# Recurrent gates split by feature chunk into two PSUM banks, with products of 32 columns

## The chip, the core and the metric

The kernel runs on one core of a Trainium2 chip. The metric is device time in microseconds. The core has a matrix engine (TensorE, PE in the profile; its weight loads are listed as PEld), a vector engine (VectorE, DVE), an activation engine (ScalarE, ACT), GpSimd (POOL) and a queue engine that issues DMAs (SyncE, SP). Matrix products are written to PSUM, an accumulation memory of banks of 2 KB per partition; the engines' other data is in SBUF. All numbers are float32.

## The reference

The input x has 8 sequences of 512 positions with 256 features. Four layers follow one another, each adding its output to its input: a mixture of experts with one shared and eight routed experts, a layer that for this depth comes to a per-sequence gain, a low-rank adapted block, and a gated recurrence. The recurrence is what the change is about. Its state has 256 features for each of the 8 sequences, and it runs over 512 positions one after the other:

```python
def step(H, xs):
    xz, xr, xh = xs
    Z = jax.nn.sigmoid(xz + H @ Whz.T + bhz)
    R = jax.nn.sigmoid(xr + H @ Whr.T + bhr)
    H_tilda = jnp.tanh(xh + R * H @ Whh.T + bhh)
    H_new = Z * H + (1.0 - Z) * H_tilda
    Y = H_new @ Whq.T + bhq
    return (H_new, Y)
```

R must be known before the candidate's product, and the candidate before the next state.

## The kernel before, in words

**Windows and steps.** The first three layers are worked in 16 windows of 32 positions (all 8 sequences, so 256 columns). Their products, activations and vector operations are jobs in lists, one for each engine. Two windows are done ahead; then the recurrence starts, and the jobs of the later windows are put between its instructions. A written planner does that while the program is built: at fixed places in each step a `jobs.fill` takes the next job that is ready by the planner's own clock (a step counts 2.43 us there). What comes out is one fixed order for each engine[...]. The recurrence's step is written out in the loop over c (32 time chunks of 16 positions) and t.

**One step.** TensorE multiplies the state by the r weights (`recur`, L1117 in `across`), then by the z weights. ScalarE applies the sigmoid to r in two parts (`gate`, L1298), one for each feature chunk of 32 columns. VectorE turns each part over in blocks of 32 by 32 (`transposed`, L1312) and multiplies by the state (L1329, s_rh). TensorE then makes the candidate's product from s_rh, ScalarE its tanh in two parts, VectorE turns each part over (d) and makes the new state with a scan, one for each chunk (L1388, s_h). z goes the same way beside this, in one part of 64 columns. ScalarE also copies each state into a history (L1402) from which the output is made later.

**Layout of the gates.** The 256 outputs of a gate lie as four strips of 32 partitions with 64 columns each. For each strip j, `across` multiplies a stationary operand of 32 columns (4 positions by 8 sequences) with 64 columns of the weights. A gate takes 2 feature chunks of the input by 4 strips, 8 products of 64 columns. In the trace each is two weight loads and two passes, so that a gate shows 16 of each.

**Banks.** r and the candidate of one time chunk share a bank, `grh`: 4 groups of 4 positions, 2 gates, 64 columns. Two such banks alternate from time chunk to time chunk. z has a third bank, `gz`, for both. Before a bank's first use `claim` (L300) writes it with eight products of zeros, so that the later products add to what is there. Then ScalarE copies the biases into it (`biases`, L1139), in two halves for r and candidate and one part for z; for the next time chunk it does so in steps 7, 8 and 9. The input's products (wx) are added by `project`: for each group of 4 positions, in four parts, r and candidate together in one product of 128 columns for each strip, z in one of 64. The parts with r and candidate stand before the candidate's products of every second step.

**Bank reuse.** The second `grh` bank first serves small products of the other layers' preparation (the ring `r_c`), and is claimed in step 4 of the first time chunk. `implied` leaves out waits that another engine's order already gives. Where ScalarE copies the z bias into the bank that z products write, the next z products do wait for it (`z_bias`).

Of the kernel before, what the change touches and what calls it, by code (L numbers as in the profile page):

```python
# [9 lines left out]
F32 = mybir.dt.float32  # L10
AF = mybir.ActivationFunctionType
ALU = mybir.AluOpType
AX = mybir.AxisListType
PSUM = bass.MemoryType.PSUM
DRAM = bass.MemoryType.DRAM

P = 128
B, T, C = 8, 512, 256
KC = C // P
# [13 lines left out]
FQ = C // NQ  # L33
GS = 4
NG = TC // GS
# [165 lines left out]
def cond_resid_kernel(  # L201
# [44 lines left out]
    def implied(later, *earlier):  # L246

        for e in earlier:
            tc.declare_no_dep(later.ins, e.ins, reason="through another engine")
# [9 lines left out]
    def pool_of(name, bufs, space=None):  # L259
        kw = {} if space is None else {"space": space}  # L260
        return ctx.enter_context(tc.tile_pool(name=name, bufs=bufs, **kw))
# [18 lines left out]
    r_xt = ring("xt", [P, KC, WS, B], 3)  # L280


    ps_g = pool_of("ps_g", 2, PSUM)
    ps_z = pool_of("ps_z", 1, PSUM)
    gz = ps_z.tile([P, 2, NG, FQ], F32, name="gz")

    def new_gates(c):
        rh = ps_g.tile([P, NG, 2, FQ], F32, name=f"grh_{c}", tag="grh")
        return rh, gz[:, c % 2]

    both = [new_gates(c) for c in range(2)]
    zeros = const.tile([P, NT], F32, name="zeros")
    nc.vector.memset(zeros, 0.0)
    rh0, rh1 = [g[0].rearrange("p n g f -> p (n g f)") for g in both]

    def claim(bank):

        for half in range(2):
            for j in range(NQ):
                nc.tensor.matmul(  # L300
                    bank[ts(j, 32), ts(half, NT)],
                    zeros[:, 0:32],
                    zeros,
                    start=half == 0,
                    stop=half == 1,
                    skip_group_check=True,
                )
# [4 lines left out]
    jobs = Jobs()  # L312
# [70 lines left out]
    r_c = Ring(None, "c", None, 1, rh1)  # L383
    pieces = {}
    for pair_ in LOW:
        for k in range(KC):
            for q in pair_:
                z = Lazy(r_w2)
                pieces[q, k] = (z, load(z, w2[ts(k, P), ts(q, R * C)], 1.0, [z]))

    wx = const.tile([P, KC, 3, C], F32, name="wx")
    wh = const.tile([P, KC, 4, C], F32, name="wh")
    for g, n in enumerate((0, 2, 1)):
        got_wx = load(wx[:, :, g, :], rows_of(sq_b[:, ts(n, C)]), 0.25)
    for j in range(NQ):
        got_wh = load(
            wh[ts(j, 32)].rearrange("q i n o -> q i (n o)"),
            sq_b[ts(j, FQ), 3 * C : 7 * C].rearrange("(i q) o -> q i o", q=32),
            0.25,
        )  # L400
# [3 lines left out]
    got_small = []  # L404
# [42 lines left out]
    for n in range(2):  # L447
        u = const.tile([P, NT], F32, name=f"u{n}")
# [285 lines left out]
    def pe(fn, deps, lazies=(), takes=0.3):  # L734
        return jobs.add("PE", fn, deps, lazies, takes)
# [7 lines left out]
    def flat(z):  # L743
# [5 lines left out]
    j = dve(  # L749
        lambda: tt(  # L750
            prod,
            rout[:, 1].rearrange("p k (o e) -> p k o e", o=1).broadcast_to([P, KC, B, E]),
            cond.rearrange("p k (b o) -> p k b o", o=1).broadcast_to([P, KC, B, E]),
            ALU.mult,
        ),
        [got_cond, got_rout],
    )
# [12 lines left out]
    j = pe(time_bias, [j], [tb_ps])  # L770
# [15 lines left out]
    for n in range(2):  # L786
        t = const.tile([P, B, 32], F32, name=f"gates{n}")
# [112 lines left out]
    mu, j = mean_over_features(cond, got_cond)  # L900
    diff = set1.tile([P, KC, B], F32, name="diff")

    def center():
# [3 lines left out]
    j = dve(center, [j], [mu], 0.4)  # L907
    dsq = set1.tile([P, KC, B], F32, name="dsq")
    j = dve(lambda: tt(dsq, diff, diff, ALU.mult), [j])
    var_ps, j = mean_over_features(dsq, j)  # L910
    var = set1.tile([P, B], F32, name="var")
    j = dve(
        lambda: nc.vector.tensor_scalar(var, var_ps.get()[:, :B], EPS_LN, None, ALU.add),
        [j],
        [var_ps],
    )

    sd0 = set1.tile([P, B], F32, name="sd0")
    j = act(lambda: nc.scalar.activation(sd0, var, AF.Sqrt), [j], (), 1.6)
# [57 lines left out]
    hid_pre, j = dense_cond(A_L2W1, lnc, V_BIAS1, "hid", got_lnc)  # L977
    hid_e, j = gated(hid_pre, AF.Erf, RSQRT2, "hid_e", j)
# [10 lines left out]
    g1_pre, j = dense_cond(A_L1W1, cond, V_B1, "g1", got_cond)  # L989
    g1, j = gated(g1_pre, AF.Sigmoid, 1.0, "g1", j)  # L990
    j = dve(lambda: tt(g1, g1, g1_pre, ALU.mult), [j])
    gate_pre, j = dense_cond(A_L1W2, g1, V_B2, "gate", j)
# [9 lines left out]
    for n, of in enumerate(LOW):  # L1002
# [59 lines left out]
            0.35,  # L1062
        )

    xts = [Lazy(r_xt) for w in range(NW)]
    l0_ends = []
    ends = [window_jobs(w, routed, xts[w], True) for w in range(2)]
# [3 lines left out]
    for w in range(2, NW):  # L1071
# [1 line left out]
            ws = list(range(EARLY * (w - 1), EARLY * w))  # L1073
            routes.append(route(ws, late_tiles, r_m, False, ends[w - 1]))
        ends.append(window_jobs(w, routes[w // EARLY], xts[w]))
    jobs.run([l0_ends[0], *got_low_in, *got_small, got_wx, got_wh])
    pro.close()


# [8 lines left out]
    with (  # L1088
# [22 lines left out]
            nc.vector.memset(s, 0.0)  # L1111
            d0s.append(s)

        def across(out, lhs, rhs, start=False):

            return [
                nc.tensor.matmul(  # L1117
                    out[ts(j, 32)],
                    lhs,
                    rhs[:, ..., ts(j, FQ)],  # L1120
                    start=start,
                    stop=False,
                    skip_group_check=True,
                )
                for j in range(NQ)
            ]

        def biases(gates):

            rh, z = gates  # L1130

            def bias(out, row):
                groups = out.shape[1]
                shape = [P, groups, *row.shape[1:]]
                if row.shape[1] == FQ:
                    row = row.rearrange("p (o f) -> p o f", o=1)
                else:
                    row = row.rearrange("p (o g) f -> p o g f", o=1)
                return nc.scalar.copy(out, row.broadcast_to(shape))  # L1139

            half = NG // 2
            return [
                lambda: bias(rh[:, :half], brow[:, RH_STORED]),
                lambda: bias(rh[:, half:], brow[:, RH_STORED]),
                lambda: bias(z, brow[:, 1]),
            ]

        def project(g, gates):

            rh, z = gates  # L1150
            n, w = g % NG, g * GS // WS
            assert all(j.done is not None for j in ends[w]), g
            x = xts[w].get()
            t0 = g * GS % WS
            parts = []
            for k in range(KC):
                xk = x[:, k, t0 : t0 + GS, :]
                parts.append(lambda k=k, xk=xk: across(rh[:, n], xk, wx[:, k, RH]))
                parts.append(lambda k=k, xk=xk: across(z[:, n], xk, wx[:, k, G_Z]))
            return parts  # L1160

        def recur(out, g, s):
            made = []
            for k in range(KC):
                made += across(out, s(k), wh[:, k, g])
            return made

        def state(u):
            return lambda k: s_h[u][:, k, :, :, 1]
# [57 lines left out]
                    queue,  # L1227
                )

        gates = both[0]  # L1230
        for part in biases(gates):
            part()
        jobs.run(ends[0])
# [36 lines left out]

        jobs.ending = lambda: l0_ends[-1].done is not None
        copying = None
        z_bias = None
        biased = []
        acted = []
        used = {}
# [4 lines left out]
        for c in range(NTC):  # L1281
            hist = hists[c]
            gates = upcoming
            for t in range(TC):
# [6 lines left out]
                def chunk(x, k):  # L1291
                    return x[:, 32 * k : 32 * k + 32]

                def gate(pre, func, name, parts=1):

                    a = acts[name][s % 2]
                    made = [
                        nc.scalar.activation(x, y, func)  # L1298
                        for x, y in (
                            [(a, pre)]  # L1300
                            if parts == 1
                            else [(chunk(a, k), chunk(pre, k)) for k in range(KC)]
                        )
                    ]
                    for ins in made:
                        implied(ins, *used.get((name, s % 2), ()))
                    used[(name, s % 2)] = list(made)
                    return a, made
# [7 lines left out]
                    used[(name, s % 2)].append(ins)  # L1316

                h = s_h[u][:, :, u, :, 1]
                made = recur(rh[:, n, 0], G_R, state(u))
                for mm in made:  # L1320
                    implied(mm, *acted, *biased)
                r, act_r = gate(rh[:, n, 0], AF.Sigmoid, "r", KC)
                if copying is not None:
                    copying(now + 1.0)
                rT = gs.tile([P, KC, GS, B], F32, name=f"rT_{s}", tag="rT")
# [23 lines left out]

                ahead = s + 5  # L1350
                part = None
                if c == 0 and t == 4:
                    claim(rh1)
                if c + 1 < NTC and t == 6:
                    upcoming = new_gates(c + 1) if c else both[1]
                    bias_parts = biases(upcoming)
                if 2 * GS <= ahead < T:
                    if ahead % GS == 0:
# [8 lines left out]
                    part()  # L1367
                    part = None
                jobs.fill("ACT", now + 1.15, 1)
                made = recur(rh[:, n, 1], G_HH, lambda k, q=s_rh[u]: q[:, k])  # L1370
                for mm in made:
                    implied(mm, *acted, *biased, *act_r)
                readers[("rh", u)] = made
                cand, act_c = gate(rh[:, n, 1], AF.Tanh, "c", KC)
                if part is not None:
                    part()
                jobs.fill("PE", now + 1.44, second_slot(s, now + 1.44))
                if bias_parts and t >= 7:
                    biased.append(bias_parts.pop(0)())
                    if not bias_parts:  # L1380
                        z_bias = biased[-1]
                else:
                    jobs.fill("ACT", now + 1.95, 1)
# [97 lines left out]
```

## Time and profile before

| What | Value |
|---|---|
| Time, median of 3 runs | 1320.2 us (1319.23 to 1321.51) |
| Profiled execution: its own time, its span | 1319.46 us, 1317.7 us |
| TensorE busy, passes | 1182.9 us (90%), 39,016 |
| VectorE busy | 914.0 us (69%) |
| ScalarE busy | 507.2 us (38%) |
| Granted TensorE clock | 0.999 |
| Passes of r, 64 columns | 8192, 225 ns each, 85.2 us idle before them |
| Passes of the candidate, 64 columns | 8192, 225 ns each, 35.3 us idle before them |
| Activations of r and of the candidate | 1024 each, 195 ns each |
| Median distance from one step's r products to the next | 2.417 us |

How to read it: the time is taken without the profile's detail and the span with it, from the first instruction to the last of one execution. A line of the page or of an answer names the engine, the line of the program, the operation, what is written from what, the shapes, and how many there were. The duration of a pass holds its latency; passes overlap, so that it is the distance of starts, not the duration, that tells how many fit into a time. A timeline line merges instructions of one kind: where they start, how long it lasts from the first start to the last end, and how many there are.

### The profile page before, as it was taken

The page shows a single profiled execution, that of the slowest core. Times are in us where ns is not written, and L with a number is a line of the kernel's source. Part 1 is how long each engine was busy: PE and PEld are TensorE (multiplying, and loading weights), DVE is VectorE, ACT ScalarE, POOL GpSimd, SP SyncE. Part 2 cuts the span into 40 slices and gives each one's busy share as a digit, 9 for nine tenths or more (in the row PEclk, how much of TensorE's full clock was granted, in tenths as well). Part 3 has the DMA queues.
Part 4 walks back from the last instruction along what each step waited for, and adds up shares of the span by engine and source line. Part 5 has one row for each costly group of instructions (what it writes and reads, how often), then busy time and mean ns, then how long its engine had stood idle before and what let it go on. Part 6 is the DMA issues. An engine that isn't in the chain of part 4 may idle for free.

```text
span 1317.7 us, 88546 instructions
## 1 busy us (share of the span) xinstructions
PE 1182.9 (90%) x39016; PEld 682.1 (52%) x39016; DVE 914.0 (69%) x6255; ACT 507.2 (38%) x3403; POOL 149.3 (11%) x228
## 2 busy tenths in 40 slices
PE   8999999998999999998888888888888888888886
PEld 4565555555555555555554445554554545545443
DVE  4267777777767677776766767676676767667665
ACT  2133444443344444344444433444343444433332
POOL 3310101111010100101011010101101010110000
PEclk9999999999999999999999999999999999999999
DMA  9910001100010000101000010000001000000111
GB/s 336 344 46 13 4 4 54 36 14 28 5 44 12 20 21 13 44 4 36 5 20 20 13 28 4 28 12 21 21 4 36 4 4 4 4 4 5 36 32 24
DMA packets 41586, 46.44 MB, mean 35 GB/s; under 512 B 27472, under 2 KB 31088, under 8 KB 40048
## 3 DMA queue, kind: packets, MB, share of 16 engines
q1 hardware_dynamic: 38304, 38.31, 9.6%
q8 instruction: 305, 5.00, 1.6%
q0 software_dynamic: 1184, 2.31, 0.5%
q14 instruction: 81, 0.66, 0.2%
q10 hardware_dynamic: 1712, 0.16, 0.1%
HBM read 36.45 MB, written 4.33 MB: 31 GB/s over the span
## 4 chain that ended last, share of the span: by engine, by line
PE 67%; DVE 19%; ACT 9%; issue 4%; DMA 0%; ACTq 0%; DVEq 0%
PE grh L1117 36%; PE hp L455 11%; PE acc L455 7%; DVE d L1312 7%; DVE rT L1312 6%; ACT c L1298 5%; PE gz L1117 5%; ACT r L1298 4%; PE low L455 4%; DVE s_h L1388 3%; PE misc L455 3%; DVE s_rh L1329 2%; PE misc L1025 1%; DMA b<-in_bias_dram 0%; ACT sig L548 0%
## 5 line engine op out<-in xcount | busy, mean ns | idle before, releaser
L1298 ACT ACTIVATE r<-grh 128x32 f32<-128x32 f32 x1024 | 146.2, 195 | 426.6 <-PE grh L1117 426.6
L1312 DVE STREAM_TRANSPOSE rT<-r 128x32 f32<-128x32 f32 x1024 | 156.0, 190 | 220.7 <-ACT r L1298 217.1
L1117 PEld LDWEIGHTS grh<-wh,s_h 128*32 128x32 f32 x8192 | 139.9, 109 | 308.7 <-DVE s_h L1388 308.7
L1117 PE MATMUL grh<-wh,s_h 128*32 128x64 f32 x8192 | 221.2, 225 | 85.2 <-DVE s_h L1388 84.9
L1298 ACT ACTIVATE c<-grh 128x32 f32<-128x32 f32 x1024 | 146.3, 195 | 308.8 <-PE grh L1117 307.8
L1117 PE MATMUL grh<-wh,s_rh 128*32 128x64 f32 x8192 | 220.9, 225 | 35.3 <-DVE s_rh L1329 10.9
L1117 PEld LDWEIGHTS grh<-wh,s_rh 128*32 128x32 f32 x8192 | 138.7, 108 | 194.6 <-DVE s_rh L1329 190.8
L1312 DVE STREAM_TRANSPOSE d<-c 128x32 f32<-128x32 f32 x1024 | 156.5, 191 | 115.8 <-ACT c L1298 109.9
L1117 PE MATMUL gz<-wh,s_h 128*32 128x64 f32 x8192 | 208.9, 219 | 0.7 <-issue 0.6
L455 PE MATMUL hp<-x,sw_sb 128*32 128x256 f32 x2016 | 153.6, 387 | 1.7 <-ACT sig L548 1.6
L1117 PEld LDWEIGHTS gz<-wh,s_h 128*32 128x32 f32 x8192 | 152.8, 110 | 1.0 <-issue 1.0
L455 PE MATMUL hp<-x,rw_sb 128*32 128x256 f32 x2016 | 150.5, 380 | 1.5 <-ACT sig L580 1.1
L596 POOL TENSOR_TENSOR g<-gl,bc 128x256 f32<-128x256 f32 x128 | 93.6, 733 | 510.8 <-DVE s_h L1388 349.4
L455 PE MATMUL acc<-g,rw_sb 128*32 128x256 f32 x2048 | 150.8, 379 | 0.7 <-issue 0.7
L1388 DVE TENSOR_TENSOR_SCAN s_h<-d,d 128x16 f32<-128x16 f32 x1024 | 145.3, 184 | 0.0
L1329 DVE TENSOR_TENSOR s_rh<-rT,s_h 128x8 f32<-128x8 f32 x1024 | 133.1, 167 | 0.0
L1312 DVE STREAM_TRANSPOSE zT<-z 128x64 f32<-128x64 f32 x512 | 121.8, 238 | 0.6 <-ACT z L1298 0.5
L1298 ACT ACTIVATE z<-gz 128x64 f32<-128x64 f32 x512 | 121.3, 237 | 0.8 <-PE gz L1117 0.8
L1117 PE MATMUL grh<-wx,xt 128*32 128x128 f32 x2048 | 106.7, 274 | 1.3 <-ACT r L1298 1.3
L1402 ACT COPY hist<-s_h 128x16 f32<-128x16 f32 x512 | 106.2, 207 | 0.5 <-DVE s_h L1388 0.5
L1341 DVE TENSOR_TENSOR d<-zT,s_h 128x16 f32<-128x16 f32 x512 | 90.6, 177 | 17.5
L1342 DVE TENSOR_SCALAR d<-zT 128x16 f32<-128x16 f32 x512 | 86.4, 169 | 0.0
(151 smaller groups left out, 1190.9 us busy)
## 6 DMA issues: line engine op xcount, KB each, us to landing
bc<-comb_d SPq DMA_DIRECT2D x56, 256.0 KB, 3.2
w<-in_w_dram SPq DMA_DIRECT2D x8, 1024.0 KB, 12.8
out_dram<-x SPq DMA_DIRECT2D x14, 256.0 KB, 2.9
x<-in_xT_dram SPq DMA_DIRECT2D x2, 1536.0 KB
rw_sb<-in_rw_dram SPq DMA_DIRECT2D x2, 1024.0 KB
bc<-comb_d POOLq DMA_DIRECT2D x8, 256.0 KB, 6.8
sw_sb<-in_sw_dram SPq DMA_DIRECT2D x3, 512.0 KB, 6.4
wsq_a<-in_sq_a_dram SPq DMA_DIRECT2D x1, 1280.0 KB
```

The lines of the kernel that those rows point to most:

```text
L455: nc.tensor.matmul(out[ts(j, 32)], lhs[:, ts(j, 32)], rhs, start=start, stop=False, skip_group_check=True,)
L596: lambda gl=gl, g=g, e=e: nc.gpsimd.tensor_tensor(g.get(), gl.get(), bcs[e // 2].get()[:, e % 2], ALU.mult),
L1025: nc.tensor.matmul(flat(gp)[ts(t, 32), :C], hid[:, r, k, :], w[:, ts(R // 2 * (t % 2) + r, C)], start=False, stop=False, skip_group_check= ...
L1117: nc.tensor.matmul(out[ts(j, 32)], lhs, rhs[:, ..., ts(j, FQ)], start=start, stop=False, skip_group_check=True,)
L1298: nc.scalar.activation(x, y, func)
L1312: ins = nc.vector.transpose(dst.rearrange("p i u b -> p i (u b)"), src.rearrange("p (i r) -> p i r", r=32),)
L1329: prod = tt(s_rh[u][:, k, u, :], rT[:, k, u, :], h[:, k], ALU.mult)
L1341: tt(d1[:, :, u, :, 1], zT[:, :, u, :], h, ALU.mult)
L1342: nc.vector.tensor_scalar(d0[:, :, :, 1], zT[:, :, u, :], -1.0, 1.0, ALU.mult, ALU.add)
L1388: new = nc.vector.tensor_tensor_scan(s_h[v][:, k, v].rearrange("p b w -> p (b w)"), d0[:, k].rearrange("p b w -> p (b w)"), d1[:, k, u].re ...
L1402: nc.scalar.copy(hist[:, :, t, :], s_h[v][:, :, v, :, 1])
```

## The change

r and the candidate move into two banks by feature chunk of the output. `grh0` holds columns 0 to 31 of each strip and `grh1` columns 32 to 63, each for both time chunks, 4 groups and 2 gates. A product of 64 columns becomes two of 32, one for each bank: for each feature chunk of the input first four strips into `grh0`, then four into `grh1`. The input's product of 128 columns becomes two of 64. The first activation of a gate reads `grh0` and waits for the products into it; the second reads `grh1` and waits for the rest. The bias copies are one for each bank, of the same size as the halves before; because the bank now also holds the time chunk at work, the r products of the next step wait for them (`rh_bias`). The second bank is needed from the start, so its claim moves from step 4 of the first time chunk to the preparation, behind the last use of that bank there (`marked`). The order of all other instructions on every engine is the same as before.

```diff
-    ps_g = pool_of("ps_g", 2, PSUM)
+    ps_g = pool_of("ps_g", 1, PSUM)
     ps_z = pool_of("ps_z", 1, PSUM)
     gz = ps_z.tile([P, 2, NG, FQ], F32, name="gz")
+    grh = [ps_g.tile([P, 2, NG, 2, 32], F32, name=f"grh{i}") for i in range(KC)]
 
     def new_gates(c):
-        rh = ps_g.tile([P, NG, 2, FQ], F32, name=f"grh_{c}", tag="grh")
-        return rh, gz[:, c % 2]
...
+        return [b[:, c % 2] for b in grh], gz[:, c % 2]
...
+    z = Lazy(r_c)
+    marked = pe(lambda z=z: claim(z.get()), [got_low_in[1]], [z], 0.9)
...
-    jobs.run([l0_ends[0], *got_low_in, *got_small, got_wx, got_wh])
+    jobs.run([l0_ends[0], *got_low_in, marked, *got_small, got_wx, got_wh])
...
-        def across(out, lhs, rhs, start=False):
-
+        def across(out, lhs, rhs, half=None):
+
+            n, at = (FQ, 0) if half is None else (32, 32 * half)
             return [
                 nc.tensor.matmul(
                     out[ts(j, 32)],
                     lhs,
-                    rhs[:, ..., ts(j, FQ)],
-                    start=start,
+                    rhs[:, ..., j * FQ + at : j * FQ + at + n],
+                    start=False,
...
-                parts.append(lambda k=k, xk=xk: across(rh[:, n], xk, wx[:, k, RH]))
+                parts.append(
+                    lambda k=k, xk=xk: [
+                        across(rh[i][:, n], xk, wx[:, k, RH], i) for i in range(KC)
+                    ]
+                )
...
         def recur(out, g, s):
+
             made = []
             for k in range(KC):
-                made += across(out, s(k), wh[:, k, g])
+                if isinstance(out, list):
+                    for i in range(KC):
+                        made += across(out[i], s(k), wh[:, k, g], i)
+                else:
+                    made += across(out, s(k), wh[:, k, g])
             return made
...
-                made = recur(rh[:, n, 0], G_R, state(u))
+                pre_r, pre_h = [[b[:, n, i] for b in rh] for i in range(2)]
+                made = recur(pre_r, G_R, state(u))
                 for mm in made:
-                    implied(mm, *acted, *biased)
-                r, act_r = gate(rh[:, n, 0], AF.Sigmoid, "r", KC)
+                    implied(mm, *acted, *(b for b in biased if b is not rh_bias))
+                rh_bias = None
+                r, act_r = gate(pre_r, AF.Sigmoid, "r")
...
-                if c == 0 and t == 4:
-                    claim(rh1)
...
                 if bias_parts and t >= 7:
                     biased.append(bias_parts.pop(0)())
-                    if not bias_parts:
+                    if bias_parts:
+                        rh_bias = biased[-1]
+                    else:
                         z_bias = biased[-1]
```

More of the change, by code (lines that the diff above doesn't have):

```diff
@@ L280, in cond_resid_kernel @@
     r_xt = ring("xt", [P, KC, WS, B], 3)
-    ps_g = pool_of("ps_g", 2, PSUM)
+    ps_g = pool_of("ps_g", 1, PSUM)
     ps_z = pool_of("ps_z", 1, PSUM)
     gz = ps_z.tile([P, 2, NG, FQ], F32, name="gz")
+    grh = [ps_g.tile([P, 2, NG, 2, 32], F32, name=f"grh{i}") for i in range(KC)]
     def new_gates(c):
-        rh = ps_g.tile([P, NG, 2, FQ], F32, name=f"grh_{c}", tag="grh")
-        return rh, gz[:, c % 2]
-    both = [new_gates(c) for c in range(2)]
+        return [b[:, c % 2] for b in grh], gz[:, c % 2]
     zeros = const.tile([P, NT], F32, name="zeros")
     nc.vector.memset(zeros, 0.0)
-    rh0, rh1 = [g[0].rearrange("p n g f -> p (n g f)") for g in both]
+    rh0, rh1 = [b.rearrange("p c n g f -> p (c n g f)") for b in grh]
     def claim(bank):
@@ L1139, in bias @@
                 return nc.scalar.copy(out, row.broadcast_to(shape))
-            half = NG // 2
             return [
-                lambda: bias(rh[:, :half], brow[:, RH_STORED]),
-                lambda: bias(rh[:, half:], brow[:, RH_STORED]),
+                *(
+                    lambda i=i: bias(rh[i], brow[:, RH_STORED, ts(i, 32)])
+                    for i in range(KC)
+                ),
                 lambda: bias(z, brow[:, 1]),
@@ L1228, in output_jobs @@
                 )
-        gates = both[0]
+        gates = new_gates(0)
         for part in biases(gates):
@@ L1272, in cond_resid_kernel @@
         copying = None
-        z_bias = None
+        rh_bias = z_bias = None
         biased = []
@@ L1292, in chunk, with gate @@
                     return x[:, 32 * k : 32 * k + 32]
-                def gate(pre, func, name, parts=1):
+                def gate(pre, func, name):
                     a = acts[name][s % 2]
@@ L1299, in gate @@
                         for x, y in (
-                            [(a, pre)]
-                            if parts == 1
-                            else [(chunk(a, k), chunk(pre, k)) for k in range(KC)]
+                            [(chunk(a, k), y) for k, y in enumerate(pre)]
+                            if isinstance(pre, list)
+                            else [(a, pre)]
                         )
@@ L1351, in cond_resid_kernel @@
                 part = None
-                if c == 0 and t == 4:
-                    claim(rh1)
                 if c + 1 < NTC and t == 6:
-                    upcoming = new_gates(c + 1) if c else both[1]
+                    upcoming = new_gates(c + 1)
                     bias_parts = biases(upcoming)
@@ L1369, in cond_resid_kernel @@
                 jobs.fill("ACT", now + 1.15, 1)
-                made = recur(rh[:, n, 1], G_HH, lambda k, q=s_rh[u]: q[:, k])
+                made = recur(pre_h, G_HH, lambda k, q=s_rh[u]: q[:, k])
                 for mm in made:
@@ L1373, in cond_resid_kernel @@
                 readers[("rh", u)] = made
-                cand, act_c = gate(rh[:, n, 1], AF.Tanh, "c", KC)
+                cand, act_c = gate(pre_h, AF.Tanh, "c")
                 if part is not None:
```

## The prediction

> **What bounds the kernel now.** I read first the chain of work that ended last, then the waits by total, then the timeline of one step.
>
> ```profile
> PE 67%; DVE 19%; ACT 9%; issue 4%; DMA 0%; ACTq 0%; DVEq 0%
> ```
>
> ```profile
> ACT r L1298 <- PE grh L1117: 426.6, 505, 7.3
> ...
> PEld grh L1117 <- DVE s_h L1388: 308.7, 511, 1.0
> ACT c L1298 <- PE grh L1117: 307.8, 501, 1.0
> ...
> PEld grh L1117 <- DVE s_rh L1329: 190.8, 480, 0.8
> ```
>
> The page says that TensorE is busy 90% of the span, and the chain puts 67% on it. That alone would suggest a TensorE bound. The waits (total us, times, longest) say otherwise: some 500 times, so once in nearly every one of the 512 recurrence steps, the weight loads of the r products wait for the state and those of the candidate products for r*h, and the activations wait for the products. It is a ring, and the ring sets the period. One trip round it, 801.39 to 803.81:
>
> ```profile
> 801.39 0.27 PEld L1117 LDWEIGHTS grh<-wh,s_h 128*32 128x32 f32 x16 [0.73 <-DVE s_h L1388]
> 801.39 0.43 PE L1117 MATMUL grh<-wh,s_h 128*32 128x64 f32 x16 [0.25 <-DVE s_h L1388]
> ...
> 801.64 0.41 PE L1117 MATMUL gz<-wh,s_h 128*32 128x64 f32 x16
> ...
> 801.86 0.61 PE L455 MATMUL hp<-x,sw_sb 128*32 128x256 f32 x8
> 801.89 0.29 ACT L1298 ACTIVATE r<-grh 128x32 f32<-128x32 f32 x2 [0.94 <-PE grh L1117]
> ...
> 802.12 0.30 DVE L1312 STREAM_TRANSPOSE rT<-r 128x32 f32<-128x32 f32 x2
> ...
> 802.29 0.40 PE L1117 MATMUL grh<-wx,xt 128*32 128x128 f32 x8
> 802.37 0.26 DVE L1329 TENSOR_TENSOR s_rh<-rT,s_h 128x8 f32<-128x8 f32 x2
> ...
> 802.59 0.43 PE L1117 MATMUL grh<-wh,s_rh 128*32 128x64 f32 x16
> ...
> 803.09 0.28 ACT L1298 ACTIVATE c<-grh 128x32 f32<-128x32 f32 x2 [0.16 <-PE grh L1117]
> 803.32 0.30 DVE L1312 STREAM_TRANSPOSE d<-c 128x32 f32<-128x32 f32 x2 [0.23 <-ACT c L1298]
> 803.56 0.28 DVE L1388 TENSOR_TENSOR_SCAN s_h<-d,d 128x16 f32<-128x16 f32 x2
> ...
> 803.81 0.43 PE L1117 MATMUL grh<-wh,s_h 128*32 128x64 f32 x16 [0.37 <-DVE s_h L1388]
> ```
>
> The step lasts 2.42 us, and 477 of the 511 steps last under 2.43 whatever lies between their products. 512 x 2.42 is 1239 of the span's 1317.7 us. So what each gate takes from its first product to its first activation counts twice a step: 801.89 - 801.39 = 0.50 us.
>
> **Pitch of the products.** A float32 product stands in the trace as two passes, and passes for the four column strips run side by side: 16 passes are four groups of four. z: (801.86 - 801.64)/4 = 55 ns a group of 64 columns; hp: (802.29 - 801.86)/2 = 215 ns for 256. The line through both is 0.833 ns a column + 2.3. The r block takes 0.25 against 0.22 for z, since its first weight load is in the open: 27 ns.
>
> **Part 1, products of 32 columns (on the path).** Each gate's 4 groups of 64 become 8 groups of 32, in the order: first feature chunk bank 0, bank 1; second chunk bank 0, bank 1. Bank 0 is complete after group 6. Let p be a group's pitch. Before, the last group starts 27 + 3 x 55.6 = 194 ns in, and the activation 306 ns later (53 of streaming, 253 fixed). After, group 6 starts 27 + 5p in, and the activation 306 - 27 = 279 ns later. The gain a gate is 194 - 5p, about zero at 39.
>
> There is no pass of 32 columns in this trace. From below, the line gives p = 29. From above, 55.6: halving a pass brings nothing. The nearest rows are weight loads, which now must keep up with half the stream. In the r block, which starts at 801.388, four loads have begun by 801.41 and eight by 801.465; by the trace the fifth follows the first by 28 ns, which is the time in which a load ends and its products start. The third line shows loads of 128 columns with products of only 8, so that the loads alone set the pace:
>
> ```profile
> 801.39 0.13 PEld L1117 LDWEIGHTS grh<-wh,s_h 128*32 128x32 f32 x4 [0.73 <-DVE s_h L1388]
> ```
>
> ```profile
> 801.39 0.16 PEld L1117 LDWEIGHTS grh<-wh,s_h 128*32 128x32 f32 x8 [0.73 <-DVE s_h L1388]
> ```
>
> ```profile
> 28.15 0.97 PEld L955 LDWEIGHTS grh<-cond,wsq_a 128*128 128x128 f32 x8 [0.41 <-issue]
> ```
>
> The last: (0.97 - 0.19, one load's duration)/7 = 111 ns for 128 columns; a quarter is 28, or 32 if 5 of the 111 are fixed. Eight instructions of a group (four loads, four passes) start at best within 27 ns. Three limits of 27 to 32 ns lie together, so I take p = 30: 194 - 150 = 44 ns a gate, 88 a step, 512 x 88 = 45.1 us.
>
> A rule speaks against this. The Trainium skill, "TensorEngine Tiling (Array Packing)", section Instruction Overhead, says that each matmul carries about 60 cycles and that a free size of 1 takes as long as 60. Read as columns, a pass of 32 costs one of 60: 60 x 0.833 + 2.3 = 52 ns, and the change costs 98 us (below). The line has only 2.3 ns beside its slope, so no such floor shows down to 64 columns; at the 2.4 GHz that the skill's "TensorE: Matmul & The Clock Gate" (its table of the spec) gives the array, 0.833 ns is two cycles, 32 columns are 64, and read as cycles the rule doesn't bind. I follow the line; the rule is the slow end.
>
> **Part 2, what the longer stream takes from TensorE.** 8p - 222 = +18 ns a gate, plus 4 for the input products, where four groups of 64 (222) replace two of 128 (218). Every second step has the input products just ahead of the candidate's: they start at 802.29, leave TensorE at 802.53, and it idles 56 ns until 802.59. 56 - 22 = 34 is less than 44, so 10 ns are lost in 256 steps: 2.6 us. Of the 1019 gate starts after 75 us, 81 had under 50 ns to spare; these I count as bound by TensorE, which lose the gain and pay the longer stream: 81 x (44 + 18) = 5.0 us. The other starts have 0.09 to 0.53 us.
>
> **Part 3, the second activation's new wait.** Bank 1 is complete 2p = 60 ns after bank 0; the second activation starts 93 ns after the first anyway (0.29 - 0.195), so nothing, up to p = 46. Behind it in ScalarE's queue are the history copy and z, whose transpose waits for s_rh on VectorE.
>
> **Part 4, bias copies and claim.** Each new bank holds both time chunks, so r products wait for a bias copy twice a chunk. Behind that wait are z and the background products. In the trace a copy (0.39 us, behind the candidate activations) ends 0.16 us before the next r products, or a little more, in all 62 cases; of this 0.06 goes to the semaphore (the first s_rh ends 0.056 before the load that waits for it). It moves with the candidate, so nothing; without that cover 62 x 0.1 = 6 us at most. The claim of the second bank leaves step 4, where that step and the next took 2.97 and 2.60, so 0.73 over 2.42, and goes to the prologue on a full TensorE, four groups of 215 = 0.86: +0.1. The other instructions keep their order on all queues, and no DMA is issued or moved. 18,432 more load-and-pass pairs lengthen instruction fetch (5.00 MB in 305 packets now, one in 4.1 us; later one in 2.8, each taking 1.6% x 16 x 1317.7/305 = 1.1 us): hidden.
>
> **Sum.** 45.1 - 2.6 - 5.0 - 0.1 = 37.4 us off the profiled 1319.5 gives 1282.1. The median of the runs shown is 0.7 higher: **1283**. In general the saving is about 221 - 6.13p us: 43 at 29, 13 at 34, nothing at 36, -24 at 40, -98 at 52.
>
> **Rivals.** (a) Pitch of 33 to 36: loads, stream and issue, all near 29, get in each other's way, and the gain shrinks to 1301 to 1320. For: they nearly coincide. Against: the block's first loads cycle in 28 ns. (b) Slower, one mechanism: a floor per pass or per load of 36 ns or more. It decides from p = 36, not 39, because the longer stream also delays the candidate in every second step. At 40 it is 1344, at 52 1418, at 55.6 1440. For: the rule, and no row of 32 columns. Against: the line and the loads. (c) The early wait doesn't bite: the first activation starts only after all eight groups, at 306 + 7p = 516 ns against 500: 17 ns a gate, 17 us, with part 2 about 1345. Against: each activation has a wait of its own on TensorE[...].
>
> **How the numbers follow.** The forecast (p 29 to 33, 1277 to 1301) gets 0.56, (a) 0.12, (b) 0.27, (c) 0.05. Under 0.2% is what a measurement here can't tell from no change; 0.04 of (a) falls within it. Faster 0.64, same 0.04, slower 0.32. The range: low is the stream limit with nothing lost in part 2, 1319.5 - 49 + 0.7 = 1272; high is p = 40, 1345, which leaves out the worst of (b), some 0.17. The likeliest case's own range is 1272 to 1302.
>
> **What would show it.** A step of 2.33 to 2.35; r block to z block 0.26 us, not 0.25; first activation 0.456 after the first product; activations still 93 apart; the candidate waiting for TensorE in every second step. Wrong if z starts 0.32 or more after r, or if bias steps or instruction fetch show gaps.

## The result and the profile after

The changed kernel takes 1711.2 us (median of 4 runs, 1710.7 to 1714.9) against 1320.4: 1.296 times as long (95% interval 1.295 to 1.298), 391 us more. The forecast was 1283, and the worst of its rivals, a pass of 32 columns that costs as much as one of 64, would have given 1440.

The page of the changed kernel: busy times, the queue that brings instructions, the chain.

```profile
PE 1314.4 (77%) x57448; PEld 874.1 (51%) x57448; DVE 932.4 (54%) x6255; ACT 537.5 (31%) x3403; POOL 148.8 (9%) x228
...
q8 instruction: 449, 7.36, 1.8%
...
PE 65%; issue 21%; DVE 9%; ACT 4%; DMA 1%; SPq 0%; ACTq 0%; POOL 0%; DVEq 0%
```

TensorE is busy for 132 us more, but its share of the span fell from 90% to 77%. "issue" in the chain rose from 4% to 21%, and 21% of 1713 is 360 us, nearly the whole loss. In that time TensorE had nothing to wait for that the profile shows. The waits of its weight loads say the same (total us, times, longest):

```profile
PEld grh L1120 <- issue: 226.6, 256, 2.6
...
PEld gz L1120 <- issue: 84.7, 76, 2.3
...
PEld hp L455 <- issue: 38.4, 45, 2.0
PEld acc L455 <- issue: 29.3, 31, 2.0
```

These, with 18.8 more at two smaller lines, make 398 us. In the kernel before the same five kinds of products waited 5.0 us so, and its largest such line is

```profile
PEld hp L455 <- issue: 2.4, 11, 0.2
```

The waits fall on whatever stands next in the queue, on products that the change didn't touch too (z, hp, acc).

Where nothing interrupts it, a gate's first activation comes earlier, as was forecast, though by less. The timeline of a candidate's gate of the changed kernel, and of an r gate one step on:

```profile
1002.33 0.46 PE L1120 MATMUL grh<-wh,s_rh 128*32 128x32 f32 x32
...
1002.80 0.29 ACT L1311 ACTIVATE c<-grh 128x32 f32<-128x32 f32 x2 [0.37 <-PE grh L1120]
...
1003.52 0.64 PE L1120 MATMUL grh<-wh,s_h 128*32 128x32 f32 x31
...
1004.17 0.29 ACT L1311 ACTIVATE r<-grh 128x32 f32<-128x32 f32 x2 [1.08 <-PE grh L1120]
```

The first has its activation 0.47 us after its first product (0.50 before the change). In the second the 32 passes are torn apart (the last of them starts at 1004.00), and it takes 0.65.

The gaps have a beat. Stretches of the changed kernel, cut at the ends of five gaps that follow one another; behind the length stand busy time and, in brackets, the number of instructions of each engine:

```profile
822.77:826.52 3.75, 2.60 (x128) 1.48 (x128) 2.53 (x17) 1.10 (x8) 0.76 (x2) 1.00 0.02 4
826.52:830.16 3.64, 3.15 (x127) 2.21 (x128) 1.87 (x13) 1.50 (x8) 0.47 (x1) 1.00 0.02 5
830.16:833.63 3.47, 2.56 (x128) 1.49 (x128) 1.98 (x13) 1.36 (x8) 0.00 (x0) 1.00 0.02 5
833.63:837.38 3.75, 2.54 (x128) 1.73 (x128) 1.86 (x14) 1.39 (x9) 0.00 (x0) 1.00 0.02 4
```

From gap to gap there are 128 loads and 128 passes (one pass is missing from the records), 256 instructions, and they take 3.5 to 3.75 us. So it is throughout: the loop has 414 such gaps before weight loads, and of the 413 distances between them 357 are exactly 256 instructions and 22 exactly 512. A packet of the instruction queue holds 7.36 MB/449 = 16.4 KB, 256 instructions of 64 bytes. 57,448 pairs are 449 packets; 39,016 before were 305. So the theory that the runs test: **TensorE's instructions arrive at about one block of 256 in 3.7 us, and the change needs them faster than that.** Its rival: the narrow passes, the two banks or their new waits are slow in themselves.

### The profile page after: what moved, and what is told of

Same layout as the page of the kernel before. It is cut to its first block, busy times and chain, and to the rows that moved or that the text cites. A ratio compares the mean times of both kernels' runs of the same rounds, so it can differ in the third digit from the quotient of the medians.

```text
span 1713.1 us, 125511 instructions
## 1 busy us (share of the span) xinstructions
PE 1314.4 (77%) x57448; PEld 874.1 (51%) x57448; DVE 932.4 (54%) x6255; ACT 537.5 (31%) x3403; POOL 148.8 (9%) x228
## 3 DMA queue, kind: packets, MB, share of 16 engines
q8 instruction: 449, 7.36, 1.8%
## 4 chain that ended last, share of the span: by engine, by line
PE 65%; issue 21%; DVE 9%; ACT 4%; DMA 1%; SPq 0%; ACTq 0%; POOL 0%; DVEq 0%
PE grh L1120 29%; PE hp L455 12%; PE gz L1120 9%; PE acc L455 8%; DVE d L1325 5%; PE low L455 4%; ACT c L1311 3%; DVE s_h L1403 2%; PE misc L455 2%; DVE rT L1325 1%; DMA bc<-comb_d 1%; ACT r L1311 0%; PE misc L1025 0%; DVE s_rh L1344 0%; DMA b<-in_bias_dram 0%
## 5 line engine op out<-in xcount | busy, mean ns | idle before, releaser
L1120 PEld LDWEIGHTS grh<-wh,s_h 128*32 128x32 f32 x16384 | 221.0, 112 | 334.5 <-DVE s_h L1403 212.9
L1120 PE MATMUL grh<-wh,s_h 128*32 128x32 f32 x16384 | 280.0, 200 | 135.2 <-issue 81.4
L1120 PE MATMUL grh<-wh,s_rh 128*32 128x32 f32 x16384 | 279.4, 199 | 111.4 <-issue 98.9
L1120 PEld LDWEIGHTS grh<-wh,s_rh 128*32 128x32 f32 x16384 | 219.5, 112 | 224.0 <-issue 110.8
L1120 PE MATMUL gz<-wh,s_h 128*32 128x64 f32 x8192 | 246.4, 224 | 53.0 <-issue 53.0
L455 PE MATMUL acc<-g,rw_sb 128*32 128x256 f32 x2048 | 167.3, 383 | 12.0 <-issue 12.0
L455 PE MATMUL hp<-x,rw_sb 128*32 128x256 f32 x2016 | 167.3, 388 | 11.0 <-issue 9.6
L1120 PE MATMUL grh<-wx,xt 128*32 128x64 f32 x4096 | 128.9, 222 | 18.4 <-issue 18.3
L1120 PEld LDWEIGHTS grh<-wx,xt 128*32 128x32 f32 x4096 | 117.8, 112 | 48.7 <-issue 21.2
L1120 PE MATMUL gz<-wx,xt 128*32 128x64 f32 x2048 | 90.9, 227 | 19.7 <-issue 19.5
```

The source lines that it names most:

```text
L455: nc.tensor.matmul(out[ts(j, 32)], lhs[:, ts(j, 32)], rhs, start=start, stop=False, skip_group_check=True,)
L1120: nc.tensor.matmul(out[ts(j, 32)], lhs, rhs[:, ..., j * FQ + at : j * FQ + at + n], start=False, stop=False, skip_group_check=True,)
```

## The experiments

**Instructions alone.** The kernel before, with nothing of the change in it, gets products of zeros onto two columns of the z bank, behind the candidate's products; 18, 9 or 4 a step:

```diff
+                for i in range(PADS):
+                    mm = nc.tensor.matmul(
+                        z[ts(i % NQ, 32), n, 0:2],
+                        zeros[:, 0:32],
+                        zeros[:, 0:2],
...
                 jobs.fill("PE", now + 1.44, second_slot(s, now + 1.44))
```

> The kernel before, with its banks, waits and 64-column products untouched, and 18 more products a step that add zeros to two columns of the z bank, behind the candidate's: 36 load-and-pass pairs a step, 57,448 in all, as many as the change has. Theory 'instruction fetch' (TensorE's queue can't bring 256 instructions faster than about once in 3.7 us): the changed kernel's time, 1680 to 1725 us, with stalls 256 instructions apart. Rival 'the narrow passes or the two banks and their waits are what is slow': none of them is here, so 1320 to 1350, the rest being some 0.25 us a step of passes in TensorE's idle time.

> The kernel before with 9 products of zeros a step: 48,236 pairs, 377 fetches. Instruction fetch: time = fetches x 3.7 us and what is outside the loop, so 1711 - 72 x 3.72 = 1443, 1425 to 1460. Rival 'each added instruction costs the same': half of pad18's loss, 1509.

> The same with 4 products a step, 43,112 pairs, 337 fetches of 256 instructions. Instruction fetch: the onset lies where fetches x 3.72 us fill the time, at about 343 fetches, so 1320 to 1335. Rival 'any further instruction costs': a ninth to a quarter of pad18's loss, 1365 or more.

| Kernel | Load-and-pass pairs | Packets of instructions | Time, us | Ratio to before, 95% interval |
|---|---|---|---|---|
| before | 39,016 | 305 | 1320.4 | 1 |
| pad4 | 43,112 | 337 | 1337.6 | 1.0125, 1.0096 to 1.0155 |
| pad9 | 48,232 | 377 | 1463.3 | 1.107, 1.089 to 1.126 |
| pad18 | 57,448 | 448 | 1697.8 | 1.285, 1.280 to 1.291 |
| the change | 57,448 | 449 | 1711.2 | 1.296, 1.295 to 1.298 |

With as many instructions as the change and none of its banks, waits or narrow gate products, 96% of the loss is there (377 of 391 us). The stretches of pad18, cut in the same way:

```profile
835.35:839.09 3.75, 3.15 (x128) 2.13 (x128) 1.69 (x13) 0.79 (x6) 0.00 (x0) 1.00 0.02 4
839.09:842.56 3.47, 2.95 (x128) 1.85 (x128) 2.25 (x16) 1.08 (x8) 0.00 (x0) 1.00 0.02 7
842.56:846.31 3.75, 2.54 (x128) 1.91 (x128) 2.36 (x15) 0.79 (x6) 1.17 (x2) 1.00 0.03 7
```

The same beat of 256. The dose is not a straight line through the kernel before: 32 packets more cost 17 us, the next 40 cost 126 and the next 71 cost 235, that is 0.5, then 3.1 and 3.3 us each. pad9 came 20 us above the figure expected and just over its range (its two runs lie 11 us apart), and pad4 3 us over its range: a packet costs 3.1 to 3.3 us beyond the onset, not 3.72, and the onset is soft, at about 330 packets. The loop of the kernel before has 4 gaps of instructions, that of pad4 35, that of pad9 231; that an uneven demand makes the onset soft is likely, but not shown. "Each added instruction costs the same" foretold 1509 for pad9 and misses by more. The kernel before had some 25 packets to spare, one in twelve.

**The change without the shortage.** To see what the split does by itself, work was left out of both kernels alike. The first pair dropped the z products, the input products and all but the first product of the background sums:

> The kernel before with work left out: no product of the state with the z weights, no input products in the loop, and of each background sum only the first product (its output is not the reference's). The chain r, candidate, state is whole. Some 75 pairs a step or fewer. Both theories: the ring still sets the period, 2.40 to 2.42 us a step, 1290 to 1315 us.

> The changed kernel with the same work left out: 75 pairs a step, so 256 instructions in more than 3.7 us at a step of 2.33. Instruction fetch: no stalls, and the early first activation is to be seen: a step shorter by 0.08 to 0.10 us than in the lean kernel before, 40 to 50 us in all, pitch of a group of four passes 29 to 30 ns. Rival 'narrow passes or the two banks are slow': the step stays above the lean kernel before's by 0.1 us or more.

1451.0 and 1362.8 us. Neither is to be compared: TensorE, now busy for 67% and 68% of the span, ran at a granted clock of 0.699 and 0.770, and in the lean kernel before the median gate had its first activation 719 ns after its first product. The pair settles nothing of the sizes; the quickest gates of the lean changed kernel already show 468 ns.

The second set made the background products as one over 128 columns instead of four strips of 32, so with a quarter of their instructions:

```diff
+        if tiles == NQ:
+            nc.tensor.matmul(
+                out, lhs, rhs, start=start, stop=False, skip_group_check=True
+            )
+            return
```

> The kernel before, with each background product of four column strips made as one product over all 128 columns (the same sums): 31,664 pairs instead of 39,016. Instruction fetch is no bound in the kernel before, so its easing alone brings nothing: 1310 to 1330 if a full-width product of 256 columns takes the 430 ns of two feature chunks' passes that four strips take; slower if full-width products, or the change between the two widths, cost more.

> The changed kernel with the same wide background products: 50,096 pairs, 391 fetches. Instruction fetch: 58 fetches fewer at 3.7 us each, so 1711 - 215 = about 1497, if the wide products cost nothing by themselves (else more by what the wide kernel before shows). Rival 'the narrow passes or the banks are slow': the gate blocks are as they were, so 1680 or more.

wide_before took 1421.4 us: the wide form costs 100 us by itself, so it is no way to save instructions here. Its trace shows where (medians): a wide pass starts 149 ns after a strip pass, where a strip pass of 256 columns starts after 36; a strip pass starts 309 ns after a wide one of 256 columns, where after a strip pass of as many it is 209; and wide passes follow one another at 216 ns at best, mostly at 320. How much of that is the wider load and how much the change of widths, no run separates. wide_after took 1566.2, 145 us less than the change with 58 packets fewer, though it has the wide products too. The rival had 1680 or more. With more left out on top of it:

> The wide kernel before with work left out: the input products in the loop, and the second feature chunk of the z product (its output is not the reference's). 23,472 pairs. TensorE stays busier than in the first lean pair, so that its clock should stay near 1. Both theories: 2.41 to 2.42 us a step, about 1310.

> The changed kernel with wide background products and the same work left out: 39,856 pairs, 311 fetches, which need 1160 us at 3.7 us each, less than the ring. Instruction fetch: no stalls, and the change's own gain: first activation 30 to 45 ns earlier a gate (pitch 29 to 32.5 ns), a step of 2.33 to 2.36 us, 30 to 45 us less than the lean kernel before of this pair. Rival 'narrow passes or banks slow': steps above 2.45.

1377.7 and 1362.4 us, 15 less instead of 30 to 45, and the two runs of lean2_before lie 11 us apart. The clock was 0.968 and 0.974. In both kernels about half of the steps are long, a quarter over 2.6 us, probably where the wide products hold TensorE. The median steps are 2.42 and 2.45 us, the lower quartiles 2.416 and 2.367. The quick half shows the gain, but a median of 2.45 is also where the rival's sign begins, so this pair alone decides nothing.

The third set keeps TensorE streaming nearly as long (busy for 85% and 88% of the span) and saves instructions by leaving out strips, and the input products in the loop:

```diff
-        for j in range(tiles):
+        for j in range(tiles if start or whole else 1):
...
-                made_z = recur(z[:, n], G_ZH, state(u))
+                made_z = []
+                for k in range(KC):
+                    made_z += across(z[:, n], state(u)(k), wh[:, k, G_ZH], strips=1)
```

> The kernel before with work left out in a third way, which keeps TensorE streaming as long but with fewer instructions: z products and all but the first product of each background sum on one column strip of four, and no input products in the loop (its output is not the reference's). 23,892 pairs. 2.41 to 2.42 us a step, about 1308 us, if the clock stays near 1.

> The changed kernel with the same left out: 40,276 pairs, 315 fetches, 1170 us at 3.7 each. Instruction fetch: nearly no stalls, first activation 468 to 470 ns after the first product (498 before), a step of 2.36, so 27 to 31 us less than the lean kernel before of this set. Rival 'narrow passes or banks slow': not less.

1316.2 and 1306.1 us, 0.9972 (0.9959 to 0.9986) and 0.9883 (0.9841 to 0.9926) of the kernel before, at clocks of 0.992 and 0.997. A candidate's gate in the timelines, first of the lean kernel before, then of the lean changed one:

```profile
800.57 0.43 PE L1125 MATMUL grh<-wh,s_rh 128*32 128x64 f32 x16
...
801.07 0.28 ACT L1306 ACTIVATE c<-grh 128x32 f32<-128x32 f32 x2 [0.69 <-PE grh L1125]
```

```profile
802.23 0.46 PE L1128 MATMUL grh<-wh,s_rh 128*32 128x32 f32 x32
...
802.70 0.29 ACT L1315 ACTIVATE c<-grh 128x32 f32<-128x32 f32 x2 [0.66 <-PE grh L1128]
```

0.50 us from first product to first activation became 0.47; over all gates the medians are 498 and 469 ns, and the median step fell from 2.417 to 2.359 us. 512 x 0.058 would be 30 us. 10 were measured. By the two traces, 9 of the missing 20 lie in steps with one of 21 gaps of instructions, which are still there at 315 packets, about 5 in the steps behind the bias copies, 2 ahead of the loop, which begins so much later, and 3 to 4 in other long steps.

The bias copies are a cost of the change itself. The r products of the next step now wait for them:

```profile
855.64 0.29 ACT L1315 ACTIVATE c<-grh 128x32 f32<-128x32 f32 x2 [0.66 <-PE grh L1128]
855.87 0.38 ACT L1150 COPY grh<-brow 128x256 f32<-128x256 f32 x1
...
856.42 0.48 PEld L1128 LDWEIGHTS grh<-wh,s_h 128*32 128x32 f32 x31 [0.80 <-ACT grh L1150]
```

This wait stands in all 31 time chunks that prepare a next one. Steps 7, 8 and 9 have medians of 2.450, 2.409 and 2.379 us against 2.359, 0.16 us a chunk together; in the lean kernel before they take 2.417 (step 9: 2.416) like the rest.

So with instructions in supply the change is faster, by about a quarter of the forecast here: the slowest of the two lean changed runs (1306.4) lies 9 us under the fastest of the seven lean runs before (1315.2). The rival, which foretold no gain, falls.

**Which bank the first activation waits for.** Last, the lean changed kernel with the loops over bank and input chunk exchanged, all into the first bank ahead of the second:

```diff
-            for k in range(KC):
-                if isinstance(out, list):
-                    for i in range(KC):
-                        made += across(out[i], s(k), wh[:, k, g], i)
+            if isinstance(out, list):
+                for i in range(KC):
+                    for k in range(KC):
+                        made += across(out[i], s(k), wh[:, k, g], i)
+                return made
```

> The same lean changed kernel, but all four groups into the first bank ahead of those into the second. If the first activation starts when its own bank is complete: the third group waits for the second chunk's state, 92 ns after the first load, and the first activation comes at 92 + 28 + 32 + 279 = 431 ns instead of 469, a step of 2.29 or less, 35 to 40 us below the lean changed kernel. If it waits for both banks in truth: no earlier than before.

1323.3 us, 17 slower than the order of the change. A step of it:

```profile
801.10 0.44 PEld L1128 LDWEIGHTS grh<-wh,s_rh 128*32 128x32 f32 x32 [0.48 <-DVE s_rh L1349]
801.10 0.55 PE L1128 MATMUL grh<-wh,s_rh 128*32 128x32 f32 x32
801.59 0.36 ACT L1316 ACTIVATE c<-grh 128x32 f32<-128x32 f32 x2 [0.34 <-PE grh L1128]
```

The two activations, 0.29 us together in the change's order, take 0.36: they start 159 ns apart, not 93, because the second bank is now complete four groups after the first, no longer two. So the second chunk is late all round the ring, and its s_rh reaches TensorE some 153 ns after the first: the third group waits for it. The first bank's last pass then starts at 227 ns, and the activation at 488. The expectation's 92 ns was wrong, since it took the spacing of the old order. Still, the activation does start on its own bank: the second bank's last pass starts only at 353 ns, 135 before the activation, while in the three lean kernels of this set the medians from the last pass needed to the first activation are 262 to 286. A gap of instructions in lean3_after shows it without arithmetic:

```profile
803.43 0.45 PE L1128 MATMUL grh<-wh,s_h 128*32 128x32 f32 x28 [0.26 <-DVE s_h L1409]
...
803.90 0.20 ACT L1315 ACTIVATE r<-grh 128x32 f32<-128x32 f32 x1 [0.90 <-PE grh L1128]
...
804.43 0.23 PE L1128 MATMUL grh<-wh,s_h 128*32 128x32 f32 x2 [0.56 <-issue]
...
804.73 0.20 ACT L1315 ACTIVATE r<-grh 128x32 f32<-128x32 f32 x1 [0.63 <-PE grh L1128]
```

28 of the 32 passes are through, the last four, of the second bank, come half a microsecond later, and the first activation goes at 0.47 us as always; only the second waits.

## Why the prediction was wrong

**The step that failed** is the last sentence of part 4: "18,432 more load-and-pass pairs lengthen instruction fetch [...] one in 2.8, each taking [...] 1.1 us): hidden." It set a packet's transfer time against the time between packets. The transfer does take 1.0 us in the changed kernel, and the queue's share of the DMA engines is 1.8%. But packets don't follow one another at 1.0 us: in the changed kernel a gap ends 1.4 us after the packet's transfer does (half of the 414 gaps 1.33 to 1.45), and even the shortest distances between packets are 3.4 us (the 5th percentile of all, median 3.6). The loop has 110 pairs a step, so that the forecast's step of 2.35 us needs a packet in 2.73 us. At 3.5 us a packet, 110 pairs are 3.01 us a step: 512 x (3.01 - 2.42) = 302 us, most of the loss of 391. On average the packets came 3.72 us apart, which accounts for the rest. The trace of before held the warning: its shortest distances (5th percentile), at a demand of one in 4.1 us, were also 3.5. The prediction's last sentence named gaps in the instruction fetch as a sign of being wrong, and they came, but it gave them no chance and no cost.

The Trainium skill's "Runtime: NRT & Kernel Launch", section Instruction fetch mechanics, gives the block of 16 KiB and 256 instructions, which this trace agrees with, and says that crossing into the next block is mostly hidden because dispatch is slower than the fill. Here it isn't: eight instructions of a group start within 27 ns, and the measurement decides.

**The other steps.**
- That the ring bounds the kernel before: borne out. The lean kernel before, with a good part of TensorE's instructions gone, keeps its step of 2.417.
- Part 1, the early activation: the mechanism holds, its size was off (medians of the lean pair of the third set). The gain is 29 to 30 ns a gate instead of 44, 58 a step instead of 88. Of the missing 15 ns a gate, 4 are in the pitch p and 10 in the term after it. Groups of four stand 31.7 ns apart in the lean changed kernel, not 30, and group 6 starts 181 ns in, not 177. The activation follows its start by 289 ns, not by 279: halving the passes was to take 27 ns from this distance and took 17. Why was not found. The pitch fits the upper reading of the row of 128-column loads (32), but no run separates the loads from the passes.
- The rule of 60 cycles: read as columns it gave 52 ns; 31.7 were measured, so read that way it doesn't hold here. The line through the longer passes (29) was the better guide.
- Part 2, what the stream takes from TensorE: not tested by itself, as the lean sets leave the input products out.
- Part 3: the second activation starts 93 ns after the first where nothing is torn, as foretold.
- Part 4, bias copies and claim: the copies were put at nothing, 6 us at most, and cost about 5 in the lean changed kernel, where the first weight load starts 0.18 us after the end of the first copy instead of the 0.06 counted on. The claim was put at 0.1; the loop begins 0.7 us later in the changed kernel and 2.0 in the lean one, and how much of that is the claim no run singles out. pad18, which has neither change, leaves 14 us of the loss for them and all else.
- Rivals: (b) had the sign, but its mechanism, a pitch of 36 ns or more, isn't there. (c) is refuted by the last run and by the gate that a gap cut in two. The fetch was not among the rivals, and that is why the range was too narrow. Its low end, 1319.5 - 49 + 0.7, is 1271 and not 1272; nothing hangs on that.

## What to carry to other kernels

Count an engine's instructions as well as its time: here TensorE could not take more than 256 in some 3.5 to 3.7 us, 27 to 29 ns a load-and-pass pair on average. When products are cut in half, the streaming changes little (here eight groups of 31.7 ns for four of 55.6) and the instructions double; divide the new count by 256, multiply by the shortest distance between instruction packets in the trace, and set that against the span before anything else. Here it would have been 449 x 3.5 = 1572 us, far over 1320. It is no exact forecast: the change took 1711, and pad4 lost 17 us though 337 x 3.5 is only 1180. "issue" in the chain and gaps of equal instruction count are how it shows.

## What was not expected of the hardware

- TensorE's instruction supply: one block of 256 in 3.4 us at best (the shortest twentieth of the packets' distances), though a block's transfer takes 1.0. What fills the rest of that time was not found; no run changed it. It goes in steps: of the 357 distances of exactly 256 instructions between gaps, 320 lie within 20 ns of 3.47, 3.745 or 4.02 us, 0.275 apart, and in pad18 375 of 390.
- Its onset is soft: 337 packets in 1338 us already cost 17 us.
- Passes of 32 columns side by side on four strips follow at 31.7 ns a group, little more than half of the 55.6 of 64 columns.
- The same sums over 128 columns instead of four strips of 32 made the kernel 100 us slower.
- Taking work from TensorE until it was busy for 67% of the span lowered its granted clock to 0.70 and made the kernel slower, 1451 us instead of 1320. At 85% the clock stayed at 0.99.
